# Cross attention: who finishes a head, and how eight PSUM banks are shared out

## The chip, the cores and the metric

The kernel runs on one core of one Trainium2 chip. The core has five engines that run side by side, each with its own queue of instructions: PE (TensorE, the matrix multiplier), DVE (VectorE), ACT (ScalarE), POOL (GpSimd) and SP (SyncE, which here issues transfers). The working memory SBUF and the accumulators of PSUM have 128 partitions; PSUM is used here as eight banks of 512 float32 values per partition. An engine takes its instructions strictly in the order of its queue; between engines, semaphores say when an input is there or a buffer is free. The metric is the device time of one execution in microseconds (us).

## What is computed

The reference adds three blocks to a residual stream of 4 x 128 tokens of width 1024: a cross attention over 4 x 2048 context tokens, a causal self attention, and a gated feed-forward network with 4-bit weights. The change lies in the cross attention, in which every one of the 512 query rows attends to all 8192 keys, with 16 heads of width 64, and in which queries, keys, values and attention weights are rounded to 8-bit steps:

```python
q = _fq_sym(q, axis=-1); k = _fq_sym(k, axis=-1); v = _fq_sym(v, axis=2)
attn = jnp.einsum('bhqd,bhkd->bhqk', q, k)
attn = jax.nn.softmax(attn.astype(jnp.float32), axis=-1)
attn = _fq_unsigned(attn, axis=-1)
out = jnp.einsum('bhqk,bhkd->bhqd', attn, v)
...
return out @ Wp + bp
```

So a head ends with three factors on the accumulated products: a constant, the scale of the values (one per column, `sv`), and one over the sum of the row's exponentials.

## The kernel before

The stage works in units: a unit is one head h and one tile t of 128 query rows, 16 x 4 = 64 units in all. A unit has eight steps, g = 0 to 7, of 1024 keys each. The order of all instructions of the stage is written out by hand, in one loop over `s` (512 steps and the 18 that the lags add), under a manual schedule. Step s = 8n + g of unit n issues, in this order:

- at g = 0 and 4, from the second unit on, `exponentials` (L849): ACT turns half a unit of scores, 4096 keys, into whole numbers from 0 to 255, and sums them into `sums`. It handles the unit before;
- `scores`: two matmuls on PE (L808) into a tile `sc` of two banks, of which there are two, and one instruction on DVE (L815) that multiplies them by the scales of the keys (`sk`), writes `e` and keeps the maximum. `e` has three buffers of half a unit;
- in the last tile of a head (t = 3): `load_keys` (SP), `spread_scales` (POOL, L788, a PARTITION_BROADCAST that fills `sk` of the next head) and, at g = 7, `load_rows` (L784, four small loads issued by POOL for the head after the next);
- at g = 7 `maximum` (L831): DVE joins the eight maxima into `m`, for which ACT's exponentials wait;
- `transposes` of the step 12 earlier (`LAG_T`), where g is 0, 1, 4 or 5: four matmuls on PE (L864) into a one-bank tile `a_pt`, and a copy of it to SBUF (L871), which ACT makes except in the last two units. The other half of the weights is transposed by DMA;
- `values` of the step 18 earlier (`LAG_V`): eight matmuls on PE (L913) that add to `av`, a bank that holds all four row tiles of a head;
- at certain steps `load_values` (L778): POOL loads the values of the next pair of heads. It does so in the last tile of an odd head (first part), and 19, 21 and 23 steps after that tile's first step (the other three parts; each waits until PE has used an older part).

`values` of the last tile of a head reaches g = 7 at step 8n + 25, which is step 1 of the unit three further on, the third tile of the next head. There DVE finishes the head: it sums `sums` (L925), takes the reciprocal (L926), multiplies `av` by the constant and `sv` (L928) and the result by the reciprocal (L936), into `xo`. Only then may PE begin to accumulate the next head, at step 2 of that unit, since `av` has one buffer; `a_pt` has three, from the same pool `at_ps`. With `sc` that makes eight banks. The last head (h = 15) ends in a tail in which the projection already begins; `xo` is read there for the first time.

Of the kernel before, what the change touches and what calls it, by code (L numbers as in the profile page):

```python
# [34 lines left out]
F32 = mybir.dt.float32  # L35
# [6 lines left out]
ALU = mybir.AluOpType  # L42
AX = mybir.AxisListType
PSUM = bass.MemoryType.PSUM
DRAM = bass.MemoryType.DRAM

P = 128
B, S, C = 4, 128, 1024
NT = B * S // P
NC = C // P  # L50
H, D = 16, 64
# [7 lines left out]
NSC = NK // SC  # L59
# [20 lines left out]
F16_UNITS = 16777216.0  # L80
# [6 lines left out]
def tile_perceiver(  # L87
# [26 lines left out]
    nc = tc.nc  # L114
# [640 lines left out]
    xo = [opool.tile([P, NT, 512], F32, name=f"xo{n}", tag=f"x{n}") for n in range(2)]  # L755
# [3 lines left out]
    with tc.tile_pool(name="at_e", bufs=1) as at_e, tc.tile_pool(  # L759
        name="at_s", bufs=4  # L760
    ) as small, tc.tile_pool(name="at", bufs=2) as at, tc.tile_pool(
        name="at_ps", bufs=3, space=PSUM
    ) as at_ps:
        sc_ps = sc_s.enter_context(tc.tile_pool(name="sc_ps", bufs=2, space=PSUM, side="right"))
        sv = small.tile([P, C], F32, name="sv", tag="sv", bufs=1)
# [24 lines left out]
            )  # L790

        units = [(h, t) for h in range(H) for t in range(NT)]
        state, avs, sums = {}, {}, {}

        def scores(n, g):

# [109 lines left out]
        def values(n, g):  # L906
            h, t = units[n]
            p, j = divmod(h, 2)
            if t == 0 and g == 0:
                avs[h] = at_ps.tile([P, NT, D], F32, name="av", tag="av", bufs=1)  # L910
            for i, aT in enumerate(state[n].pop(("aT", g))):
                c, k = divmod(g * (SC // P) + i, KT // NKC)
                nc.tensor.matmul(  # L913
                    avs[h][:, t, :],
                    lhsT=aT,
                    rhs=vqs[p, c][:, k, ts(j, D)],
                    start=(g == 0 and i == 0),
                    stop=(g == NSC - 1 and i == SC // P - 1),
                )
            if g < NSC - 1:  # L920
                return
            del state[n]
            if t == NT - 1:
                r = small.tile([P, NT], F32, name="r", tag="r")
                nc.vector.tensor_reduce(r, sums[h], AX.X, ALU.add)  # L925
                nc.vector.reciprocal(r, r)  # L926
                o = xo[h // 8][:, :, ts(h % 8, D)]
                nc.vector.scalar_tensor_tensor(  # L928
                    o,
                    avs[h],  # L930
                    F16_UNITS,
                    sv[:, ts(h, D)].unsqueeze(1).to_broadcast([P, NT, D]),
                    ALU.mult,
                    ALU.mult,
                )
                nc.vector.tensor_tensor(  # L936
                    o, o, r.unsqueeze(2).to_broadcast([P, NT, D]), ALU.mult
                )
# [73 lines left out]
        with tc.manual_schedule():  # L1012
            for s in range(n_steps + LAG_V):
                n, g = divmod(s, NSC)
# [9 lines left out]
                if n < len(units):  # L1024
                    h, t = units[n]
# [13 lines left out]
                if at_step(s - LAG_V):  # L1039
                    values(*at_step(s - LAG_V))  # L1040
# [303 lines left out]
    with tc.manual_schedule():  # L1344
# [10 lines left out]
        for h, (w, n) in enumerate(PARTS):  # L1355
# [20 lines left out]
            for t in range(NT):  # L1376
                g = s + GROUP * t
# [64 lines left out]
    with tc.tile_pool(name="ff_shim", bufs=1) as ff_shim, tc.tile_pool(  # L1442
        name="ff_t", bufs=2
# [37 lines left out]
        with tc.tile_pool(name="ff_g", bufs=2) as ff_g:  # L1481
# [13 lines left out]
            with tc.tile_pool(name="g_ps", bufs=2, space=PSUM) as g_ps, tc.tile_pool(  # L1495
                name="u_ps", bufs=2, space=PSUM
# [17 lines left out]
        with tc.tile_pool(name="ff_h", bufs=1) as ff_h, tc.tile_pool(  # L1514
            name="y_ps", bufs=1, space=PSUM
# [135 lines left out]
```

## Time and profile before

Three runs took 2800.32, 2805.59 and 2807.35 us. The profiled execution took 2801.17 us, its span (from the first to the last instruction) is 2799.3 us, and its mean granted TensorE clock 0.988.

| | us |
|---|---|
| median of the runs | 2805.59 |
| profiled execution | 2801.17 |
| its span | 2799.3 |
| PE busy | 2607.1 (93%) |
| DVE busy | 2411.7 (86%) |
| ACT busy | 1262.7 (45%) |
| POOL busy | 469.8 (17%) |
| cross attention, DVE's first score step to its last | 1471.6 to 2100.4 |

A row of a timeline gives the start in us from the beginning of the span, the duration, the engine, the line, the operation, output<-inputs with their shapes, how many instructions are merged, and in brackets the idle time of the engine before it and who ended that. A row of a group gives the count, then the busy time in us and the mean duration in ns, then the idle time before the group's instructions and who ended most of it. Rows of one line give minimum, median and maximum durations in ns, and the first and the last start. PEld is the loading of weights into PE. On DVE, the records of two instructions in sequence can overlap; the distance of their starts is what a step costs.

### The profile page before, as it was taken

Reading aid. Unit: us, or ns where it says so; the run is one execution under the profiler, and the core shown is the slowest. Engines: PE = TensorE matmul, PEld = TensorE weight load, DVE = VectorE, ACT = ScalarE, POOL = GpSimd, SP = SyncE. Lnnn points to the kernel's source line nnn. Section 1 sums busy time; section 2 is a strip of 40 time slices with the busy share of each in tenths; the row PEclk is TensorE's granted clock in tenths of the full one; section 3 lists DMA queues with packets and bytes.
Section 4 is the critical chain, followed back from the end, with each engine's and each line's share of the span. In section 5 each row is a group of like instructions: output and inputs, shape, how many; then the busy total and the mean of one; then the engine's idle time right before and its main releaser. Section 6 shows DMA issues by size and latency. Waiting matters only on the chain.

```text
span 2799.3 us, 41119 instructions
## 1 busy us (share of the span) xinstructions
PE 2607.1 (93%) x15496; PEld 2054.1 (73%) x15496; DVE 2411.7 (86%) x3963; ACT 1262.7 (45%) x1404; POOL 469.8 (17%) x615
## 2 busy tenths in 40 slices
PE   8999999999999999999997877777778899899998
PEld 4888888888888888888874555555555677788887
DVE  7999999565799999999879999999996898886685
ACT  4211111121323333333218999999994244333332
POOL 0111122000012222222122333233312010000000
PEclk9999999999999999999998999999999999999999
DMA  6655565222447777777436898887874221122222
GB/s 201 190 204 196 196 222 205 97 98 98 139 123 202 195 196 189 199 188 193 126 88 145 162 172 167 159 162 151 170 147 150 79 84 62 60 96 100 95 95 97
DMA packets 450328, 412.66 MB, mean 147 GB/s; under 512 B 354889, under 2 KB 359561, under 8 KB 450129
## 3 DMA queue, kind: packets, MB, share of 16 engines
q1 hardware_dynamic: 401984, 249.86, 36.6%
q0 software_dynamic: 47088, 159.12, 17.6%
q8 instruction: 122, 2.00, 0.3%
q10 hardware_dynamic: 1056, 1.05, 0.2%
q14 instruction: 78, 0.63, 0.1%
HBM read 220.14 MB, written 104.34 MB: 116 GB/s over the span
## 4 chain that ended last, share of the span: by engine, by line
PE 69%; DVE 24%; issue 5%; ACT 2%; DMA 1%; DVEq 0%; SPq 0%; ACTq 0%
PE kv_a L353 32%; PE kv_b L353 16%; DVE e L815 16%; PE y_a L1538 3%; PE gate_a L169 3%; PE up_a L169 3%; PE acc_a L1164 2%; PE q_ps L303 2%; PE up_b L169 1%; PE gate_b L169 1%; PE y_b L1538 1%; PE acc_b L1164 1%; DVE sw_l L162 1%; PE a_pt L864 1%; PE sc L808 1%
## 5 line engine op out<-in xcount | busy, mean ns | idle before, releaser
L353 PE MATMUL kv_a<-w_h,c_h 128*128 128x512 f32 x2048 | 798.4, 390 | 0.0
L353 PE MATMUL kv_a<-w_l,c_l 128*128 128x512 f32 x2048 | 797.8, 390 | 0.6 <-ACT w_l L252 0.6
L353 PE MATMUL kv_b<-w_d,c_d 128*128 128x512 f32 x2048 | 798.0, 390 | 0.4 <-DVE c_d L163 0.4
L815 DVE CUSTOM_DVE_ANT_0 e<-sc,sk 128x1024 f32<-128x1024 f32 x512 | 593.0, 1219 | 7.0 <-PE sc L808 6.0
L849 ACT ACTIVATE a<-e,m,sqs 128x4096 int16<-128x4096 f32 x128 | 490.3, 3831 | 19.2 <-DVE m L831 19.2
L353 PEld LDWEIGHTS kv_a<-w_l,c_l 128*128 128x128 f32 x2048 | 384.8, 188 | 80.6 <-ACT w_l L252 1.0
L353 PEld LDWEIGHTS kv_b<-w_d,c_d 128*128 128x128 f32 x2048 | 384.7, 188 | 80.4 <-DVE c_d L163 0.8
L353 PEld LDWEIGHTS kv_a<-w_h,c_h 128*128 128x128 f32 x2048 | 384.7, 188 | 79.5 <-issue 0.2
L159 ACT ACTIVATE c_h<-c_raw 128x1024 fp32r<-128x1024 f32 x128 | 135.4, 1058 | 375.7 <-PE kv_a L353 365.5
L367 DVE SCALAR_TENSOR_TENSOR f<-kv_a,bkv 128x512 f32<-128x512 f32 x256 | 176.0, 687 | 147.3 <-PE kv_a L353 147.1
L808 PE MATMUL sc<-kt,qT 64*128 64x512 bf16 x1024 | 206.3, 395 | 97.3 <-DVE mx L815 95.7
L606 ACT CAST kst<-kT 128x512 bf16<-128x512 int16 x128 | 89.2, 698 | 295.7 <-DMA kT<-ki 295.4
L864 PE MATMUL a_pt<-ident,a 128*128 128x128 f32 x1024 | 173.4, 293 | 26.0 <-ACT a L849 23.5
L368 DVE SCALAR_TENSOR_TENSOR f<-kv_b,f 128x512 f32<-128x512 f32 x256 | 177.1, 692 | 19.1
L788 POOL PARTITION_BROADCAST sk<-sk_row x120 | 142.4, 1298 | 303.6 <-DVE mx L815 303.5
L864 PEld LDWEIGHTS a_pt<-ident,a 128*128 128x128 f32 x1024 | 111.1, 144 | 92.4 <-ACT a L849 54.1
L808 PEld LDWEIGHTS <-qT 64*128 64x128 bf16 x1024 | 72.2, 93 | 125.5 <-issue 96.9
L163 DVE SCALAR_TENSOR_TENSOR c_d<-c_l,c_raw 128x1024 fp32r<-128x1024 f32 x128 | 156.6, 1223 | 2.3
L162 DVE TENSOR_TENSOR c_l<-c_raw,c_h 128x1024 fp32r<-128x1024 f32 x128 | 155.8, 1217 | 1.8 <-ACT c_h L159 1.8
L162 DVE TENSOR_TENSOR fw_l<-fw_raw,fw_h 128x1024 fp32r<-128x1024 f32 x64 | 78.3, 1224 | 91.3 <-ACT fw_h L159 91.3
L375 ACT ACTIVATE va<-f 128x1024 f32<-128x1024 f32 x64 | 68.0, 1062 | 171.8 <-DVE f L368 166.2
L159 ACT ACTIVATE fw_h<-fw_raw 128x1024 fp32r<-128x1024 f32 x64 | 67.8, 1060 | 165.6 <-PE y_a L1538 69.5
(214 smaller groups left out, 4111.1 us busy)
## 6 DMA issues: line engine op xcount, KB each, us to landing
c_raw<-in_ctxT SPq DMA_DIRECT2D x128, 512.0 KB, 3.6
v_d<-f POOLq DMA_DIRECT2D x64, 512.0 KB, 3.1
vl<-v_d POOLq DMA_DIRECT2D x64, 512.0 KB, 4.2
gu_d<-w_ffn POOLq DMA_DIRECT2D x44, 512.0 KB, 3.0
fw_raw<-gu_d SPq DMA_DIRECT2D x42, 512.0 KB, 3.2
k_d<-kst POOLq DMA_DIRECT2D x128, 128.0 KB, 3.5
vq_d<-vq POOLq DMA_DIRECT2D x32, 512.0 KB, 5.0
kt<-k_d SPq DMA_DIRECT2D x64, 256.0 KB, 3.7
```

The source lines that it names most:

```text
L159: nc.scalar.mul(hi, src, 1.0 - 0.5 / UP)
L162: nc.vector.tensor_tensor(lo, src, hi, ALU.subtract)
L163: nc.vector.scalar_tensor_tensor(df, lo, -1.0 - UP, src, ALU.mult, ALU.add)
L169: nc.tensor.matmul(ps, lhsT=lhs(i, k), rhs=rhs(i, k), start=(k == 0 and i != 1), stop=(k == NC - 1 and i != 0),)
L353: nc.tensor.matmul(ps, lhsT=tokens[s][i][:, k, :], rhs=w3[s < KT][k][i][:, ts(n, 512)], start=(k == 0 and i != 1), stop=(k == NC - 1 and i ...
L367: nc.vector.scalar_tensor_tensor(f, a, 1.0 + 1.0 / UP, bias[s < KT][n], ALU.mult, ALU.add)
L368: nc.vector.scalar_tensor_tensor(f, b, -1.0 / UP, f, ALU.mult, ALU.add)
L788: nc.gpsimd.partition_broadcast(tile_of_scales(h, g), sks_at[h][32 * c : 32 * c + 1, ts(half, SC)], channels=P)
L808: nc.tensor.matmul(ps[:, ts(i, 512)], lhsT=qT[rows, h, ts(t, P)], rhs=kts[h, g // 2][rows, ts(g % 2, 512)], start=True, stop=True,)
L815: nc.vector.tensor_tensor_reduce(out=state[n]["e"][-1][:, ts(g % (NSC // NEC), SC)], in0=ps, in1=sks_at[h, g], scale=1.0, scalar=LOWEST, o ...
L849: nc.scalar.activation(a, st["e"][c], AF.Exp, bias=st["m"], scale=sqs[:, 0, t, h : h + 1], accum_out=sums[h][:, t, c : c + 1],)
L864: nc.tensor.transpose(pt[:, i, :], a[:, at_word + P * i : at_word + P * i + P], ident)
```

## The change

Except for the last head, a head is now finished by three engines. When `values` of the last tile has done half of its steps (g = 3), POOL adds the two sums of `sums`; two steps later (g = 5) DVE takes the reciprocal; at g = 7 ACT multiplies `av` by the constant into `xo`, and POOL multiplies `xo` in place by `sv` and then by the reciprocal. The last head is finished by DVE as before. `at_ps` has two buffers of each tile in place of three, and `av` no longer asks for one: two banks for `av`, two for `a_pt`. In the changed file the sum on POOL stands in line 923, the reciprocal in 925, the multiplication on ACT in 931, the products on POOL in 932 and 935.

```diff
-        name="at_ps", bufs=3, space=PSUM
+        name="at_ps", bufs=2, space=PSUM
...
-        state, avs, sums = {}, {}, {}
+        state, avs, sums, rs = {}, {}, {}, {}
...
-                avs[h] = at_ps.tile([P, NT, D], F32, name="av", tag="av", bufs=1)
+                avs[h] = at_ps.tile([P, NT, D], F32, name="av", tag="av")
...
+            if t == NT - 1 and g == NSC // 2 - 1:
+                rs[h] = small.tile([P, NT], F32, name="r", tag="r")
+                if h < H - 1:
+                    nc.gpsimd.tensor_tensor(rs[h], sums[h][:, :, 0], sums[h][:, :, 1], ALU.add)
+            if t == NT - 1 and g == NSC // 2 + 1 and h < H - 1:
+                nc.vector.reciprocal(rs[h], rs[h])
             if g < NSC - 1:
                 return
             del state[n]
-            if t == NT - 1:
-                r = small.tile([P, NT], F32, name="r", tag="r")
+            if t == NT - 1 and h < H - 1:
+                o = xo[h // 8][:, :, ts(h % 8, D)]
+                nc.scalar.mul(o, avs[h], F16_UNITS)
+                nc.gpsimd.tensor_tensor(
+                    o, o, sv[:, ts(h, D)].unsqueeze(1).to_broadcast([P, NT, D]), ALU.mult
+                )
+                nc.gpsimd.tensor_tensor(
+                    o, o, rs[h].unsqueeze(2).to_broadcast([P, NT, D]), ALU.mult
+                )
+            elif t == NT - 1:
+                r = rs[h]
                 nc.vector.tensor_reduce(r, sums[h], AX.X, ALU.add)
```

## The prediction

> **What bounds the kernel now.** I read the page first, then the groups of the cross attention's stretch alone (1472 to 2102 us of the span), then timelines. All that the change touches lies in that stretch of some 630 us. I count in steps (one tile of 1024 keys), units (eight steps: one head, one row tile; 64 of them) and heads (four units).
>
> ```profile
> L815 DVE CUSTOM_DVE_ANT_0 e<-sc,sk 128x1024 f32<-128x1024 f32 x512 | 593.0, 1219 | 7.0 <-PE sc L808 6.0 <-ACT a L849 0.9
> L849 ACT ACTIVATE a<-e,m,sqs 128x4096 int16<-128x4096 f32 x126 | 482.7, 3831 | 19.2 <-DVE m L831 19.2
> ...
> L913 PE MATMUL av<-vq,aT 128*128 128x64 f16 x1984 | 101.1, 195 | 17.5 <-DVE xo L928 17.5
> ```
>
> DVE sets the pace: its largest group idles 7.0 us in 630. But ACT, with exponentials and copies, idles only 19.2 us, so it is 3% behind. PE waits 17.5 us for the old finish to read the single `av` bank. DVE's timeline at the end of a head:
>
> ```profile
> 1690.27 1.22 DVE L815 CUSTOM_DVE_ANT_0 e<-sc,sk 128x1024 f32<-128x1024 f32 x1
> ...
> 1691.41 0.16 DVE L925 TENSOR_REDUCE r<-sum 128x4 f32<-128x8 f32 x1
> 1691.61 0.18 DVE L926 RECIPROCAL r<-r 128x4 f32<-128x4 f32 x1
> 1691.70 0.39 DVE L928 SCALAR_TENSOR_TENSOR xo<-av,sv 128x256 f32<-128x256 f32 x1
> 1692.13 0.43 DVE L936 TENSOR_TENSOR xo<-xo,r 128x256 f32<-128x256 f32 x1
> 1692.47 1.22 DVE L815 CUSTOM_DVE_ANT_0 e<-sc,sk 128x1024 f32<-128x1024 f32 x1
> ```
>
> Steps follow each other every 1.144 us; the finish holds the next one back from 1691.41 to 1692.47, 1.06 us. A unit without it takes 9.42 us (units start at 1660.85 and 1670.27). ACT's rhythm:
>
> ```profile
> 1660.96 3.80 ACT L849 ACTIVATE a<-e,m,sqs 128x4096 int16<-128x4096 f32 x1 [0.72 <-DVE m L831]
> ...
> 1664.76 1.05 ACT L871 COPY aT<-a_pt 128x512 int32<-128x512 int32 x2
> 1665.70 3.81 ACT L849 ACTIVATE a<-e,m,sqs 128x4096 int16<-128x4096 f32 x1
> ...
> 1670.44 3.82 ACT L849 ACTIVATE a<-e,m,sqs 128x4096 int16<-128x4096 f32 x1
> ```
>
> One exponential and two copies take 4.74 us, a unit 9.48: 0.06 more than DVE's plain unit. The 1.06 us of the finish is what lets ACT catch up once a head.
>
> **The change, part by part.**
>
> *Finish off DVE.* 15 heads x 1.06 = -15.9 us. The reciprocal stays; its own 0.09 to 0.18 us falls in the wait of the next part and costs nothing there (2 us in all without that cover).
>
> *Two banks for the transposes.* PE transposes half a unit when its exponential is done, at steps 4 and 5; ACT copies the results only after the *next* exponential. With three banks the first transposes of a half find a free one; with two they need the first copy behind the exponential that they wait for anyway. PE's timeline:
>
> ```profile
> 1569.90 0.66 PE L864 MATMUL a_pt<-ident,a 128*128 128x128 f32 x4 [0.35 <-ACT a L849]
> ...
> 1570.72 0.39 PE L808 MATMUL sc<-kt,qT 64*128 64x512 bf16 x2
> ```
>
> The exponential awaited here started at 1565.93: 3.97 us from its start to the transposes, 0.14 more than its length of 3.83. The copy starts 3.80 after the exponential and takes 0.56 at least (median 0.605); with the same 0.14 the bank is free at 4.50. Next scores 0.82 after the transposes (1570.72 - 1569.90), their end 0.39 later, DVE 0.04 after that (1578.50 + 0.61 against 1579.15 at its one wait in that stretch): DVE can begin step 5 at 4.50 + 1.25 = 5.75 after the exponential's start, which is 0.11 after the unit's (1660.96 - 1660.85), so at 5.86. It is due at 5 x 1.144 = 5.72. So each unit grows by 0.14, or 0.19 with the median copy; the later half has 0.1 to spare. I take 0.15 x 62 = +9.3. Bounds: 0 if PE's wait ends otherwise than I think, 0.28 x 62 = 17 with the longest copy (0.70).
>
> *The multiplication on ACT.* No row shows it. Two 512-wide copies take 0.94 us, so 256 columns take 0.24; it delays the following exponential of the finishing unit by that, and about 0.2 of it comes through to step 1 of the next unit: 15 x 0.2 = +3.0. Its own wait, for PE's last values, is hidden: these are issued at the unit's step 1, and ACT comes to it 4.7 us into the unit. Bounds 0 and 15 x 0.6 (a whole 512-wide ACTIVATE, 597 ns) = 9.
>
> *GpSimd's part, and what comes with it.* The two products on POOL (half of L1106's 1.3 us each) are read only by the projection; they cost nothing. But in the changed program's list POOL has an extra entry, ISA, ahead of L923 and again ahead of the next head's first L788, 15 and 14 times. The program before has one ahead of L1106, and the trace shows what it is:
>
> ```profile
> 2110.03 0.29 POOL masks.py:30 TENSOR_SCALAR_AFFINE_SELECT mask<-mask 128x128 bf16<-128x128 bf16 x1
> ...
> 2118.72 5.13 POOL L1106 TENSOR_TENSOR x<-x,row 128x512 f32<-128x512 f32 x4 [8.39 <-issue]
> ```
>
> ```profile
> L1106 POOLq MODIFY_POOL_CONFIG  x2: 11/11/11, 2110.4 to 2110.4; - x2
> ```
>
> POOL went from the configuration of the broadcasts to that of TENSOR_TENSOR and began its first one 8.36 us later, with no releaser for the wait. The same turn, in the same direction, now comes once a head, and DVE's reciprocal, two steps behind the sum, stands in DVE's queue behind it; behind the reciprocal stand the next unit's scores, and PE behind them. In an even head the turn begins after the four row loads and the sum is ready some 7 us early. In an odd head POOL's queue has a load of values ahead of it, which waits for PE:
>
> ```profile
> 1564.47 0.55 POOL L778 DMA_DIRECT2D vq<-vq_d  x1 [9.30 <-PE av L913]
> ```
>
> It ends at 1565.02; the unit before which the reciprocal stands starts at 1570.44, 5.42 later. A turn of 8.36 and about 0.2 for the sum and its signal (the smallest POOL rows are 0.1 to 0.3) make the reciprocal 3.1 late. The waits of the two parts above lie inside it (0.3), so 2.8 x 7 odd heads = +19.6. Bounds: 0 (the first MODIFY_POOL_CONFIG of the trace, at 1.2 us, is followed by its instruction within 0.1), and the slowest load of the trace, 11.4 us (`x<-in_x`), if heavier traffic makes the turn that slow: (11.4 + 0.2 - 5.42 - 0.3) x 7 = 41. I take 8.36, the same turn on the same engine.
>
> The Trainium skill's GPSIMD Engine Reference, section "Instruction dispatch", puts the first call of a freshly loaded kernel at 5.95 us, with no instruction visible. The trace's 8.36 us is longer. With 5.95 the reciprocal would be 0.4 late in place of 2.8, 3 us in all, and the sum below would end 17 us lower.
>
> The turn back starts when the products are done, some 7 us into the finishing unit, and holds the next head's broadcasts until 15.3. They must then run into the maximum at the unit's end, as odd heads' do now:
>
> ```profile
> 1702.64 8.25 POOL L788 PARTITION_BROADCAST sk<-sk_row  x7
> 1708.88 0.73 DVE L831 CUSTOM_DVE_ANT_0 mx<-mx,sqs 128x8 f32<-128x8 f32 x1
> ```
>
> The maximum takes 0.73 us there in place of 0.23. Seven even heads more: +3.6, between 0 and a whole broadcast each (9).
>
> *Clock and tail.* DVE's 13 waits for `sc` (6.0 us) come mostly right after PE's wait for `av`, where the granted clock falls (0.91 from 1552 to 1592 us, 1.00 in the next 40). About 5 us of it follow six such waits, 0.9 us each. They go (-5); the seven stalls of 3 us leave PE idle as long, at the same 0.9 each (+6): +1, between -5 and +12. In the tail the fourth of the last transposes, at 2114.87, would wait for a copy that ends at 2114.97: +0.3.
>
> Sum: -15.9 + 9.3 + 3.0 + 19.6 + 3.6 + 1 + 0.3 = +20.9. The profiled execution took 2801.2 us (span 2799.3 and 1.9 around it), so 2822; the median of the three runs is 4.4 above it, so I forecast **2826**.
>
> **Rivals.**
>
> *The turn is hidden* (takes under 5.4 us, so the reciprocal never waits). For: the first turn of the trace, and L548's, whose cost lies under a wait for DVE. Against: 8.36 us at L1106. Sum -15.9 + 9.3 + 3.0 + 3.6 - 5 + 0.3 = -4.7: about 2801, not slower.
>
> *Faster:* the turn is hidden and PE also absorbs the second bank (its light steps leave 0.4 us free each). Then 9.3 and 3.6 fall away too: -17.6, about 2788. Against: ACT's 9.48 us a unit, which alone eats most of it, and PE's transposing step of 1.14.
>
> *Much slower:* both turns last so long that DVE waits for the broadcasts of an odd head as well. The last one ends at 7 us (products done) plus the turn plus 8 x 1.18 plus 0.6 (a load between them) from the start of the finishing unit; DVE needs it two units of 9.6 and seven steps later, at 27.2. That decides from a turn of 10 us on. At 11.4 they are 1.3 late, 9 us in seven heads, and the reciprocals cost 41 in place of 19.6: sum +51, about 2857. Against it: POOL's 303.5 us of waiting for DVE in that stretch.
>
> **How the numbers follow.** Likeliest case 0.62, its own range 2812 to 2842; hidden turn 0.20; faster 0.07; much slower 0.11. The range 2800 to 2852 takes in most of the hidden turn and the lower part of the much slower case. What a measurement can tell from no change is about 0.3%, 8.4 us: slower 0.72, same 0.20, faster 0.08.
>
> **What would show it.** Right: TENSOR_TENSOR `r<-sum` starting 6 to 9 us after MODIFY_POOL_CONFIG; DVE idle some 3 us before RECIPROCAL in odd heads only, with POOL as the releaser; plain units of 9.55 to 9.6 us; transposes ended by ACT `aT` and no longer by `a`; no PE wait for `xo`. Wrong: RECIPROCAL without idle time before it (hidden turn), plain units of 9.42 (banks cost nothing), DVE waiting for `sk` broadcasts (much slower).

## The result, and the profile after

The changed kernel takes 2834.99 us (median of four runs, 2832.08 to 2847.32) against 2806.07 us of the kernel before (2800.32 to 2807.35): a ratio of 1.0115, 95% interval 1.0082 to 1.0149. It is 29 us slower; the forecast was 2826 us. The profiled execution took 2836.9 us with a span of 2835.0, 35.7 us more than the span before. Of these, 33.0 lie between the first and the last score step of the cross attention (661.8 us where it was 628.8); what lies behind the last step moves between 699 and 705 us from kernel to kernel without a pattern, so I compare stretches.

The groups of that stretch in the changed kernel (busy time in us, mean in ns, then the idle time before the group and who ended it):

```profile
L815 DVE CUSTOM_DVE_ANT_0 e<-sc,sk 128x1024 f32<-128x1024 f32 x512 | 597.1, 1220 | 29.1 <-PE sc L808 25.5 <-ACT a L849 0.9
L849 ACT ACTIVATE a<-e,m,sqs 128x4096 int16<-128x4096 f32 x126 | 480.3, 3812 | 39.2 <-DVE m L831 30.7 <-DMA aT_d<-a 8.0
...
L864 PEld LDWEIGHTS a_pt<-ident,a 128*128 128x128 f32 x1000 | 113.1, 149 | 135.2 <-ACT aT L871 98.6 <-issue 33.9 <-ACT a L849 2.7
L913 PE MATMUL av<-vq,aT 128*128 128x64 f16 x1984 | 104.7, 198 | 0.0
...
L831 DVE CUSTOM_DVE_ANT_0 mx<-mx,sqs 128x8 f32<-128x8 f32 x63 | 15.3, 243 | 2.3
...
L923 POOL TENSOR_TENSOR r<-sum 128x4 f32<-128x4 f32 x15 | 2.9, 192 | 118.6 <-issue 104.0 <-ACT a L849 7.6 <-ACT aT L871 7.0
L925 DVE RECIPROCAL r<-r 128x4 f32<-128x4 f32 x15 | 2.6, 175 | 21.5 <-POOL r L923 21.5
```

Four things are to be read here. The accumulator's second bank works: PE no longer waits before its products (17.5 us before, 0.0 now), and PE's transposes are released by ACT's copies `aT` in place of the exponentials `a`. The reciprocal on DVE waits 21.5 us for GpSimd. GpSimd stands still for 104.0 us, 8.0 us on average at each of 13 sums, with no releaser: the turn of its configuration. (The average hides two lengths: from MODIFY_POOL_CONFIG to the sum it is 7.0 to 7.4 us in the even heads, where the row loads stand ahead, and 8.3 to 8.9 us in the odd ones, where a load of values does.) And DVE's score steps wait 25.5 us for PE in place of 6.0, while ACT's exponentials have a wait that the kernel before did not have: 8.0 us for `aT_d<-a`, the DMA transposes.

The first such place, on GpSimd and on DVE:

```profile
1566.47 0.54 POOL L778 DMA_DIRECT2D vq<-vq_d  x1 [11.30 <-PE av L913]
1575.63 0.19 POOL L923 TENSOR_TENSOR r<-sum 128x4 f32<-128x4 f32 x1 [8.61 <-issue]
```

```profile
1573.71 0.23 DVE L831 CUSTOM_DVE_ANT_0 mx<-mx,sqs 128x8 f32<-128x8 f32 x1
...
1575.85 0.18 DVE L925 RECIPROCAL r<-r 128x4 f32<-128x4 f32 x1 [1.91 <-POOL r L923]
1575.97 1.23 DVE L815 CUSTOM_DVE_ANT_0 e<-sc,sk 128x1024 f32<-128x1024 f32 x1
```

In an odd head the load of values waits for PE until 1566.47, the turn starts behind it, GpSimd stands still for 8.61 us, and the reciprocal, ready to run since 1573.94, and all score steps behind it wait (1.9 us here). It happens in seven odd heads and in no even one, 21.5 / 7 = 3.1 us each.

The wait that I had not foreseen, on ACT (unit 8, head 2):

```profile
1549.34 3.80 ACT L849 ACTIVATE a<-e,m,sqs 128x4096 int16<-128x4096 f32 x1
...
1553.13 1.05 ACT L871 COPY aT<-a_pt 128x512 int32<-128x512 int32 x2
1557.12 3.80 ACT L849 ACTIVATE a<-e,m,sqs 128x4096 int16<-128x4096 f32 x1 [2.93 <-DMA aT_d<-a]
```

The second exponential wants to overwrite a tile that a DMA transposes is still reading. In the same window, 1540 to 1560 us, the line of the DMA transposes (minimum, median, maximum in ns that SP spends on one) reads, in the changed kernel and then in the kernel before:

```profile
L880 SPq DMA_TRANSPOSE aT_d<-a x4: 1919/3550/8157, 1539.0 to 1556.8; - x4
```

```profile
L880 SPq DMA_TRANSPOSE aT_d<-a x4: 1804/2058/4605, 1539.3 to 1555.6; - x4
```

One transposes holds SP for 8.16 us, and its tile comes free late. This befell units 8, 40 and 56 of this execution; they took 13.79, 12.98 and 13.69 us where 9.42 was usual, +12.2 in all. (A unit's length is the distance on DVE between its first step and the next unit's.)

### The profile page after: what moved, and what is told of

Its sections match the earlier page's. It is cut to its first block, busy times and chain, and to the rows that moved or that the text cites. A ratio compares the mean times of both kernels' runs of the same rounds, so it can differ in the third digit from the quotient of the medians.

```text
span 2835.0 us, 41210 instructions
## 1 busy us (share of the span) xinstructions
PE 2625.3 (93%) x15496; PEld 2058.7 (73%) x15496; DVE 2401.4 (85%) x3918; ACT 1268.3 (45%) x1419; POOL 496.0 (17%) x660
## 3 DMA queue, kind: packets, MB, share of 16 engines
q0 software_dynamic: 47088, 159.12, 18.2%
## 4 chain that ended last, share of the span: by engine, by line
PE 71%; DVE 13%; issue 9%; DMA 3%; ACT 3%; POOL 0%; ACTq 0%; DVEq 0%; SPq 0%; POOLq 0%
PE kv_a L353 30%; PE kv_b L353 15%; DVE e L815 5%; PE a_pt L864 4%; PE y_a L1553 3%; PE gate_a L169 3%; PE up_a L169 3%; PE acc_a L1179 2%; PE sc L808 2%; PE q_ps L303 2%; ACT aT L871 1%; DMA aT_d<-a 1%; PE up_b L169 1%; PE gate_b L169 1%; PE y_b L1553 1%
## 5 line engine op out<-in xcount | busy, mean ns | idle before, releaser
L815 DVE CUSTOM_DVE_ANT_0 e<-sc,sk 128x1024 f32<-128x1024 f32 x512 | 597.1, 1220 | 29.1 <-PE sc L808 25.5
L808 PE MATMUL sc<-kt,qT 64*128 64x512 bf16 x1024 | 212.6, 408 | 80.4 <-DVE mx L815 77.9
L864 PE MATMUL a_pt<-ident,a 128*128 128x128 f32 x1024 | 180.6, 302 | 68.9 <-ACT aT L871 65.9
L808 PEld LDWEIGHTS <-qT 64*128 64x128 bf16 x1024 | 66.3, 94 | 111.9 <-issue 82.1
```

Of the source, the lines that this page charges most:

```text
L808: nc.tensor.matmul(ps[:, ts(i, 512)], lhsT=qT[rows, h, ts(t, P)], rhs=kts[h, g // 2][rows, ts(g % 2, 512)], start=True, stop=True,)
L815: nc.vector.tensor_tensor_reduce(out=state[n]["e"][-1][:, ts(g % (NSC // NEC), SC)], in0=ps, in1=sks_at[h, g], scale=1.0, scalar=LOWEST, o ...
L864: nc.tensor.transpose(pt[:, i, :], a[:, at_word + P * i : at_word + P * i + P], ident)
```

## The experiments

All ratios are to the kernel before, run on the same chip. "Stretch" is the cross attention in the profiled execution.

| kernel | median, us | ratio (95% interval) | stretch, us |
|---|---|---|---|
| before | | 1 | 628.8 |
| changed | 2834.99 | 1.0115 (1.0082 to 1.0149) | 661.8 |
| two banks alone | 2810.16 | 1.0026 (1.0012 to 1.0040) | 632.1 |
| changed, sum early | 2815.56 | 1.0031 (1.0012 to 1.0051) | 640.5 |
| before, load late | 2817.44 | 1.0052 (1.0035 to 1.0069) | 636.2 |
| changed, load early | 2829.94 | 1.0092 (1.0069 to 1.0116) | 652.6 |
| changed, both early | 2805.73 | 1.0004 (0.9992 to 1.0017) | 627.6 |
| changed, no turns | 2800.68 | 0.9996 (0.9984 to 1.0008) | 621.5 |
| three banks, two halves | 2852.66 | 1.0175 (1.0156 to 1.0195) | 674.1 |
| before, two halves | 2806.11 | 1.0002 (0.9990 to 1.0013) | 628.3 |
| before, turn added | 2818.11 | 1.0052 (1.0032 to 1.0073) | 651.8 |
| before, turn added ahead | 2809.26 | 1.0015 (1.0005 to 1.0025) | 626.5 |
| short finish | 2797.05 | 0.9979 (0.9970 to 0.9988) | 621.6 |
| short finish, load early | 2793.26 | 0.9961 (0.9949 to 0.9973) | 616.2 |

**Two banks alone.**

```diff
-        name="at_ps", bufs=3, space=PSUM
+        name="at_ps", bufs=2, space=PSUM
...
-                avs[h] = at_ps.tile([P, NT, D], F32, name="av", tag="av", bufs=1)
+                avs[h] = at_ps.tile([P, NT, D], F32, name="av", tag="av")
```

> The kernel before with two banks each for accumulator and transposes, and nothing else: the whole finish stays on VectorE, GpSimd never changes its configuration. My theory, the second bank lengthens each plain unit of the cross attention from 9.42 to about 9.6 us (ACT copy to PE transposes to scores), and the waits for the accumulator's bank (0.9 us in seven odd heads) go: some 46 units x 0.17 = +8, -6, so 2808 us and no unit over 11 us. Rival 1, the 0.2 us a unit in the changed kernel comes from the work moved to ACT and GpSimd: plain units stay at 9.42, 2800 us. Rival 2, the late exponentials in units 8, 40 and 56 (about 4 us each) come from the rhythm of two banks: they appear here too, 2820 us.

Its groups:

```profile
L815 DVE CUSTOM_DVE_ANT_0 e<-sc,sk 128x1024 f32<-128x1024 f32 x512 | 596.1, 1220 | 8.1 <-PE sc L808 5.7 <-ACT a L849 0.9
...
L913 PE MATMUL av<-vq,aT 128*128 128x64 f16 x2048 | 104.1, 194 | 0.0
```

The first units of a head take 9.61 us, the second ones and the fourth ones of even heads 9.50, the others are as long as before, and no second exponential is late that was not late before. So the 0.2 us of the first units belongs to the banks, the late transposes do not, and the price of the banks net of the accumulator's wait is 7 us (0.26% of 2803); in the profiled execution 3.3 us of it lie in the stretch. Both rivals fall. One expectation missed: units of over 11 us did not go. Besides unit 1 (11.4 us in every kernel), units 2, 38 and 42 took 11.0, 11.3 and 11.4 us behind waits of DVE for `sc`. These waits come to 5.7 us as against 6.0 in the kernel before, although PE waits for no accumulator at all. So they are not, or not only, the price of the accumulator's.

**Changed, sum early.** The tile `r` and the sum move from g = 3 to g = 0, ahead of the load c = 1 in GpSimd's queue.

```diff
-            if t == NT - 1 and g == NSC // 2 - 1:
+            if t == NT - 1 and g == 0:
                 rs[h] = small.tile([P, NT], F32, name="r", tag="r")
```

> The changed kernel with GpSimd's sum issued three steps earlier, ahead of the second load of values in GpSimd's queue. My theory, the turn of the configuration costs DVE time only because in odd heads it queues behind that load, which waits for PE: the turn now begins after the row loads, as in even heads, the reciprocal's wait falls from 21.5 us to under 1, units 9, 17, ... 57 from 12.7-13.3 to about 9.6, and with the low-clock windows behind them 25 us go: 2810 us; the three late exponentials stay. Rival, the turn begins only when the sum's own inputs are there, or the reciprocal waits for something else: the wait stays near 3 us in each odd head, 2832 us or more.

```profile
L849 ACT ACTIVATE a<-e,m,sqs 128x4096 int16<-128x4096 f32 x128 | 488.3, 3815 | 25.8 <-DMA aT_d<-a 10.0 <-DVE m L831 9.9 <-issue 5.4
...
L925 DVE RECIPROCAL r<-r 128x4 f32<-128x4 f32 x15 | 2.6, 173 | 0.0
```

The wait of 21.5 us is gone altogether, and units 9, 17, ... 57 are 9.6 us long, but for one of 10.8. The late transposes stayed, in three units of this execution (15.4 us at the longest). A turn whose start is not held up by a load costs the reciprocal nothing; behind the row loads it is shorter as well (6.7 to 7.6 us in the odd heads, where it was 8.3 to 8.9).

**Before, load late,** and **changed, load early.** The first load of the next pair's values is moved in the two kernels in opposite directions.

```diff
-                if 0 <= pair < NP - 1 and since in (0, LAG_V + 1, LAG_V + 3, LAG_V + 5):
+                if 0 <= pair < NP - 1 and since in (2, LAG_V + 1, LAG_V + 3, LAG_V + 5):
```

> The kernel before with one edit: the first load of a pair's values is issued two steps later in the t=3 unit of odd heads, some 4.8 us into the unit where it was 2.45 (4.3 to 4.5 in the changed kernel). My theory for the late exponentials of units 8, 40 and 56, the turn back delays this load so that the second DMA transposes of the unit run into it: their issue grows from 1.8-3.8 us to 3-8 us here too, and where it passes 5.3 us the next unit's second exponential is late: 0 to 4 us in each of seven heads, 2816 us with half of them. Rival, the lateness needs the turn itself or the two banks: issue stays under 4 us, 2806 us.

```diff
+                if 0 <= pair < NP - 1 and since == 0:
+                    load_values(pair + 1, 0)
                 if n < len(units):
                     h, t = units[n]
                     scores(n, g)
...
-                if 0 <= pair < NP - 1 and since in (0, LAG_V + 1, LAG_V + 3, LAG_V + 5):
+                if 0 <= pair < NP - 1 and since in (LAG_V + 1, LAG_V + 3, LAG_V + 5):
```

> The changed kernel with the first load of a pair's values issued one place earlier, ahead of the broadcasts and so ahead of the turn back. My theory, the load no longer meets the second DMA transposes of the unit: their issue falls from 3.2-8.2 us to under 4, units 8, 40 and 56 from 13-13.8 to about 9.6 us, 12 us go: 2823 us; the reciprocal's wait of 21 us stays. Rival, the lateness is the turn's or the two banks': it stays, 2835 us.

In the kernel before with the late load:

```profile
L849 ACT ACTIVATE a<-e,m,sqs 128x4096 int16<-128x4096 f32 x128 | 489.9, 3828 | 25.9 <-DVE m L831 22.5 <-DMA aT_d<-a 3.3
```

In the changed kernel with the early load:

```profile
L849 ACT ACTIVATE a<-e,m,sqs 128x4096 int16<-128x4096 f32 x128 | 487.6, 3810 | 29.1 <-DVE m L831 28.4
...
L925 DVE RECIPROCAL r<-r 128x4 f32<-128x4 f32 x15 | 2.6, 175 | 22.0 <-POOL r L923 22.0
```

The late load brings ACT's wait for the transposes into a kernel that has neither turn nor second bank (units 16, 24 and 40 with second exponentials at 5.4, 7.1 and 5.7 us, and 6.3 us longer together). The median is 14 us higher; how much of that the late transposes make in the other executions, no trace shows. The early load takes it out of the changed kernel: units 8, 16, ... 56 are all 9.60 or 9.61. So the cause of the late units 8, 40 and 56 is the place of this load: GpSimd issues it behind the first broadcast, and the turn back puts that broadcast off. The reciprocal's wait is untouched, as expected. The stretch shrank by 9.2 and not by 12, because the maximum now met the broadcasts (18.2 us in its group as against 15.6; see below).

**Changed, both early,** the two moves together.

> The changed kernel with both moves: GpSimd's sum ahead of the second load of values, and the first load of values ahead of the broadcasts. My theory, the two losses are separate and add up: no reciprocal waits over 0.2 us, no second exponential later than 5.2 us into its unit; against the changed kernel's 2835 some 23 us go with the reciprocal's wait and 12 with the late exponentials, and the maximum meets the broadcasts in some heads as it did where the loads came early (+2 to +4): 2803 us, level with the kernel before. Rival, one loss hides the other or the turn costs something else as well: 2812 us or more.

No reciprocal waits, and units 8, 16, ... 56 are 9.6 us, but for unit 48 (11.1 us, with two waits for `sc` and no late exponential). In one place (units 34 and 35, away from the moved load) exponentials were late by up to 2.3 us: ACT waits there for the DMA transposes again (2.9 us), of which one held SP for 9.62 us, next to the loads c = 2 and 3. Why there and not in the other odd heads stays open. The two losses add up, and the change as such, freed of them, is level with the kernel before.

**Changed, no turns.** Sum and reciprocal on DVE at g = 5; GpSimd's products of heads 0 to 13 in one go behind its last broadcast.

```diff
-                    nc.gpsimd.tensor_tensor(rs[h], sums[h][:, :, 0], sums[h][:, :, 1], ALU.add)
...
+                nc.vector.tensor_reduce(rs[h], sums[h], AX.X, ALU.add)
                 nc.vector.reciprocal(rs[h], rs[h])
...
+                if s == NSC * NT * (H - 1) + 1:
+                    for h in range(H - 2):
+                        products(h)
```

> The changed kernel's two banks and its multiplication on ACT, but no turn of GpSimd's configuration within the 15 heads: sum and reciprocal on VectorE, and all of GpSimd's products in one go behind its last broadcast (step 481). My theory, without turns there is neither a wait of the reciprocal nor a late load: the finishing units fall from 10.48 to about 9.7, plain ones stay near 9.6: against the kernel with two banks alone (ratio 1.0026) 15.9 us of finish go, 15 x 0.25 for sum and reciprocal and 15 x 0.2 for ACT come back: 9 us less, 2800 us. Rival, ACT's extra work is dearer than that and sets units of 9.8 or more throughout: 2815 us.

The finishing units are 9.43, those with sum and reciprocal 9.81, plain ones 9.61; the stretch is 10.6 us shorter than with two banks alone, where I expected 9. ACT's multiplication is cheap.

**Three banks, two halves.** As without turns, but three banks for the transposes and both accumulators in one bank; and the kernel before with only the two halves.

```diff
-                avs[h] = at_ps.tile([P, NT, D], F32, name="av", tag="av")
+                if not avs:
+                    av2 = at_ps.tile([P, 2, NT, D], F32, name="av", tag="av", bufs=1)
+                    avs.update((i, av2[:, i % 2]) for i in range(H))
```

> As the one without turns, but three banks for the transposes as before, and the two accumulators as the two halves of one bank. My theory, this gives every gain of the change without its costs: no wait for the accumulator (-6), finish off VectorE (-15.9), sum and reciprocal on VectorE (+3.8), ACT's multiplication (+3), and units of ACT's 9.48 in place of 9.42 where the finish no longer lets ACT catch up (+0.06 x 46 = +2.8): -12, 2791 us, faster than both. Rival 1, two accumulators in one bank make PE wait for ACT's read as one accumulator does: some 2 us of PE wait in each head, 2805 us or more. Rival 2, ACT bounds the stage at once: same as the kernel before.

> The kernel before with its accumulator doubled into two halves of the same bank, the finish as it was on VectorE. It prices the accumulator's waits alone. My theory, 17.5 us of PE waiting for the finish cost the time only the 0.9 us of the units that follow in some heads (units of 11.3 in place of 10.48): these fall to 10.48, 6 us go, 2797 us. Rival, the waits are hidden and the longer units have another cause: units of 11.3 us remain, no change.

With ACT as the reader:

```profile
L924 PE MATMUL av<-vq,aT 128*128 128x64 f16 x1952 | 104.2, 199 | 52.5 <-ACT xo L941 52.5
```

Both theories of mine fell. PE waits 3.5 us in each of 15 heads before it writes one half while ACT still has to read the other, and the kernel is 49 us slower than the one before; with DVE as the reader PE waits 17.4 us, just as with one accumulator, so the price of that wait is not told apart here. The wait is one that the program puts there: both halves are one tile in one bank. The Trainium skill's page "PSUM — Partial Sum Buffer", section "PSUM bank collisions raise a hardware error", gives a reason for such a guard: it is to go by bank and quadrant, not by address, since a write of TensorE and a read by another engine in one bank and quadrant at once is an error. No run here shows the error itself, nor whether the wait goes by the tile or by the bank. What the runs show is why the change needs a bank of its own for the second accumulator once ACT, with its longer queue, does the reading.

**Before, turn added,** and **added ahead.** GpSimd's sum is added to the kernel before, into a tile that nobody reads; the second time at g = 0.

```diff
+            if t == NT - 1 and g == NSC // 2 - 1 and h < H - 1:
+                extra = small.tile([P, NT], F32, name="extra", tag="extra")
+                nc.gpsimd.tensor_tensor(extra, sums[h][:, :, 0], sums[h][:, :, 1], ALU.add)
```

> The kernel before with GpSimd's sum added at the place where the changed kernel has it, into a tile that nobody reads: 15 turns to TENSOR_TENSOR's configuration and 14 back, and nothing waiting for them; no product follows, so the turn back begins some 8 us before the next head's first broadcast. My theory, a turn costs time only through what is queued behind it and needed: the broadcasts and the first load of values start where they did (1.3 and 2.5 us into the unit), DVE waits for no GpSimd, 2804 us within 3. Rival, the turn itself slows the other engines or the DMA transposes: 2812 us or more.

```profile
L913 PE MATMUL av<-vq,aT_d 128*128 128x64 f16 x2016 | 104.4, 197 | 13.5 <-DMA vq<-vq_d 13.5
L913 PE MATMUL av<-vq,aT 128*128 128x64 f16 x2024 | 103.5, 195 | 20.8 <-DVE xo L931 18.0 <-DMA vq<-vq_d 2.8
```

A miss: 15 us slower though nobody waits for the sum. I had looked at the broadcasts and the first load only. The loads of values c = 2 and 3 stand behind the turn as well and were issued 4 to 7 us late, and PE waited 16.3 us for them, 7.9 at the longest; besides, the maximum met the broadcasts at worse moments (22.1 us in its group as against 18.1).

> The kernel before with the unread sum on GpSimd as in the run with the turn alone, but three steps earlier, ahead of the loads of values c = 1 to 3 in GpSimd's queue. In that run (ratio 1.0052) the loads stood behind the turn and PE waited 16 us for them, and the maximum met the broadcasts at a worse moment. My theory, the turn itself slows nothing, all of its cost came through GpSimd's queue: PE waits under 1 us for values, the broadcasts start 1.3 to 1.5 us into the unit, and only the maximum of the odd heads stays at 1.0 in place of 0.73 us because the first load's issue is 0.17 us longer behind a turn (+2): 2806 us, ratio 1.001. Rival, the turns slow other engines or the DMA transposes while they last: 2813 us or more.

```profile
L913 PE MATMUL av<-vq,aT_d 128*128 128x64 f16 x2032 | 100.9, 193 | 0.0
...
L831 DVE CUSTOM_DVE_ANT_0 mx<-mx,sqs 128x8 f32<-128x8 f32 x64 | 20.2, 316 | 2.3
```

With the turn ahead of the loads PE waits for no values, the broadcasts start 1.4 us into the unit, and the maximum's 20.2 us in place of 18.1 are the 2 us expected. 29 turns cost little by themselves (0.15%, 4 us, of which the maximum makes 2); they cost what they hold up in GpSimd's queue.

**Short finish,** alone and with the early load. Banks as before; on DVE sum and reciprocal at g = 5 and one product with the accumulator; the product with `sv` on GpSimd behind its last broadcast.

```diff
+            if t == NT - 1 and g == NSC // 2 + 1:
+                rs[h] = small.tile([P, NT], F32, name="r", tag="r", bufs=H)
+                nc.vector.tensor_reduce(rs[h], sums[h], AX.X, ALU.add)
+                nc.vector.reciprocal(rs[h], rs[h])
...
+                nc.vector.scalar_tensor_tensor(
+                    xo[h // 8][:, :, ts(h % 8, D)],
+                    avs[h],
+                    F16_UNITS,
+                    rs[h].unsqueeze(2).to_broadcast([P, NT, D]),
+                    ALU.mult,
+                    ALU.mult,
+                )
```

> The kernel before, banks as they were and no turn: sum and reciprocal on VectorE two steps before the end of the head, then one product with the accumulator (0.39 us) on VectorE; the other product, with sv, on GpSimd behind its last broadcast. My theory: 0.43 us of VectorE go in 15 heads, -6.5, and the accumulator is read 0.3 us sooner, so that PE's waits shrink from 17.5 to about 13 us, with 1 to 3 us of time: 2796 us. Rival, the 1.06 us of the finish is what lets ACT catch up, and units lengthen as much as the finish shortens: 2804 us.

> As the short finish, with the first load of values ahead of the broadcasts as well. My theory, the maximum's 0.73 us in odd heads is a wait for the broadcast that runs then, and the load's issue between the first two broadcasts is what sets their phase: with the load ahead the maximum falls where it does in even heads, 0.23 us: 7 x 0.5 = 3.5 us less than the short finish, 2792 us. Rival, the maximum is slow there for another reason: stays at 0.73, 2796 us.

```profile
L831 DVE CUSTOM_DVE_ANT_0 mx<-mx,sqs 128x8 f32<-128x8 f32 x64 | 14.6, 228 | 2.3
```

Both came as expected, 6 and 10 us faster than the kernel before; the second is the fastest kernel of the study (0.9961). One detail missed: PE's wait for the accumulator is 16.3 us and not 13. The early load takes the maximum from 0.73 us in odd heads to 0.23 in all.

## Why the prediction was right, and where it was not

The sign held, and so did the main cause: +21 on the profiled execution was forecast, +35.7 came, and the medians are 29 apart. Two errors, in the terms of the maximum (6 us too much) and of the clock (6 too little), cancel by luck; most of the difference that is left lies in a wait that the prediction did not have. By its terms:

- *Finish off DVE, -15.9:* right. Undisturbed finishing units fell from 10.48 to 9.42, by 1.06; the reciprocal itself puts 0.1 back in heads without a wait.
- *The reciprocal's wait, +19.6:* right in place, cause and size: 3.1 us in seven odd heads. The turn took 8.3 to 8.9 us in these heads against 8.36 taken from the row of the tail; the 5.95 us of the page that I had cited was too short here. The experiment with the sum early shows the cause, since it only moves the sum, and with it the turn, ahead of the load.
- *Two banks, +9.3, and ACT's multiplication, +3.0:* right in mechanism, somewhat high. In the run with two banks alone units grow by 4.5 us together and not by 9.3: the first ones by 0.19 each, the second ones and the even heads' fourth ones by 0.07, the others not at all, where 0.15 was taken for every unit. The multiplication took 0.40 us on ACT and not 0.24. What the other terms leave of the 33.0 us is some 10 us for banks, multiplication and reciprocals together. The eight plain first units of even numbers 4, 12, ... 60 went from 9.43 (once 9.47) to 9.61 or 9.62; the finishing units of even heads show none of it.
- *The maximum, +3.6:* the step "The turn back ... holds the next head's broadcasts until 15.3. They must then run into the maximum" failed, in sign as well. The turn back took 5.8 us and not 8.4, and it held back the broadcasts in the odd heads' last units, not in even ones: after an odd head the products are done early (ACT multiplies 1.1 to 2.8 us into the unit and not 4.8), because ACT runs ahead while DVE waits. With the sum early, where DVE does not wait, ACT multiplies 4.8 us into the unit in all heads, and the even heads' broadcasts start late too (1.8 to 3.5 us into the unit; 1.4 in the changed kernel). Shifted by 1.9 us, the broadcasts missed the maximum in six heads of seven where they had met it, so the group fell from 18.1 to 15.6 us: -2.5.
- *What was missing:* the same step followed the broadcasts and forgot the load of values that stands behind the first of them. That load came 1.9 us later and met the DMA transposes: +12 in three heads of this execution, the largest error of the sum.
- *Clock, +1:* mis-sized. With the early load, where no transposes are late, DVE's waits for `sc` are 13.2 us against 6.0 in the kernel before: +7 where I took +1. Behind the seven stalls themselves they are 10.2 us, 1.5 us a stall where I took 0.9. That the old waits would go (-5) is not borne out: with two banks alone, where PE waits for no accumulator, 5.7 us of waits for `sc` remain. The granted clock of the stretch, in the kernel before and in the changed one (us, then busy time of PE, PEld, DVE, ACT and POOL, then the clock, the DMA engines' share and GB/s):

```profile
1470.00:2100.00 630.00, 492.22 (x5976) 339.25 (x5976) 619.75 (x1210) 600.07 (x501) 192.70 (x218) 0.97 0.82 160
```

```profile
1470.00:2100.00 630.00, 482.98 (x5642) 325.53 (x5642) 577.62 (x1101) 574.04 (x490) 219.09 (x260) 0.92 0.84 154
```

Of the rivals, the hidden turn is what the sum-early run makes of the reciprocal's wait; the much slower case did not come, because no turn reached the 10 us from which it was to begin.

Why the three units and not all seven were hit is open. The load's place differs by 0.2 us between the heads (4.25 to 4.47 us into the unit) and the transposes' issue goes from 3.2 to 8.2 us; the latest loads were not always the worst.

## What to carry to other kernels

An operation given to an engine that is idle for most of the time is not free: look at everything that stands in that engine's queue, DMA issues among them, and ask what each of them holds up when it comes some microseconds later. Where an engine needs a turn of its configuration between two kinds of work, put all work of the rarer kind in one place, or start the turn ahead of any instruction that has to wait. Finishing work that only a much later stage reads can be put off to where the queue is empty: the short finish, which does that with the product with `sv` and leaves the rest on DVE (0.9979), was faster than every kernel here that turns GpSimd once a head.

## What the runs showed of the hardware

The maximum, an operation of DVE with two inputs in SBUF, waits for the running broadcast to end. GpSimd's broadcasts follow each other every 1.16 us (three merged rows of 3.62), and in the changed kernel's unit 47 the maximum started just before the second began:

```profile
1965.89 3.62 POOL L788 PARTITION_BROADCAST sk<-sk_row  x3
...
1967.01 1.22 DVE L831 CUSTOM_DVE_ANT_0 mx<-mx,sqs 128x8 f32<-128x8 f32 x1
```

The broadcasts start at 1965.89, 1967.05 and 1968.21; the maximum ends at 1968.23, with the start of the third, and takes 1.22 us for 0.23 us of work. In all runs the rule is the same: a maximum that starts up to 0.94 us behind a broadcast's start ends 0.02 us behind the start of the next one, one that starts 0.96 to 1.1 us behind it is not held (0.23 us). So its cost, 0 to 1 us, hangs on the phase of the two engines alone, and moves with any edit ahead of the broadcasts. The score steps, with one input in PSUM, are not held: their mean is 1218 to 1220 ns in all kernels. The Trainium skill's page "SBUF — State Buffer", section "SBUF: two separate sides", states this lock, for VectorE with two SBUF inputs against a GpSimd operation that reads SBUF, and that it is held for the whole instruction; the runs agree but for the last 0.2 us, in which the maximum could already start.

The turn of GpSimd's configuration has no fixed length, and its direction alone does not set it. Back to the broadcasts it took 5.6 to 5.9 us in the odd heads of the changed kernel, with only GpSimd's own products ahead of it, but 7.9 to 9.1 us, seven times, behind two loads of values in the run "before, turn added". The first of each, in the changed kernel (DVE, which the row names, was done 1.9 us before; the last row is the load of values that stands behind the first broadcast) and with the turn added:

```profile
1536.07 0.61 POOL L935 TENSOR_TENSOR xo<-xo,r 128x256 f32<-128x256 f32 x1
1542.70 1.30 POOL L788 PARTITION_BROADCAST sk<-sk_row  x1 [6.01 <-DVE mx L815]
1543.85 0.74 POOL L778 DMA_DIRECT2D vq<-vq_d  x1
```

```profile
1574.93 1.28 POOL L778 DMA_DIRECT2D vq<-vq_d  x2
1584.81 8.28 POOL L788 PARTITION_BROADCAST sk<-sk_row  x7 [8.60 <-issue]
```

To TENSOR_TENSOR it took 8.3 to 8.9 us in the changed kernel behind a load of values and 7.0 to 7.4 us behind the row loads; in the sum-early run, behind the row loads in all heads, 6.7 to 7.7 us. So in both directions the longest turns are those with loads of values just ahead. Behind one such load the turn to TENSOR_TENSOR took 8.2 to 8.9 us and the turn back 6.2 to 7.1 us ("changed, load early"), so the direction may count as well. By what way a load lengthens a turn, no run shows.
